# A decoder layer on one core: tile 2's first scores beside tile 1, the first block's last rows on ScalarE, tile 6's products before the rest of tile 7's scores

## The chip, the core and the metric

The kernel runs on one core of a Trainium2 chip. The core has five engines that work side by side, each through its own queue of instructions and in the order of that queue: TensorE (matrix products; PE in the profile, its weight loads PEld), VectorE (DVE), ScalarE (ACT), GpSimd (POOL) and SyncE (SP), which here only issues loads. An instruction waits at the head of its queue until the semaphores that it names have been raised by other engines or by transfers (DMA), and everything behind it waits too. The metric is the device time of one execution in microseconds (us), lower is better.

## What is computed

Two batches of 512 rows of 1024 features pass three sub-layers. Each adds its result to its input and normalises the row (mean 0, variance 1).

```
# attention per row over its own 32 x 32 (d, e) scores, 8 groups
q = einsum('bse,edh->bsdh', x, Wq) + bq ; k, v alike with 8 heads, repeated 4 times
scores = einsum('bsdh,bseh->bsde', q, k) / sqrt(32)
out = einsum('bsde,bseh->bsdh', softmax(scores), v).reshape(...)
x = _layernorm(x + out)
# product with the context, both rounded to 0..255 codes
q1, q2 = fake_quant(x, ...), fake_quant(ctx_4096, ...)
x = _layernorm(x + matmul(q1, q2))
# feed-forward: 2048 hidden columns, 512 latent ones scaled by the two largest gate values
h = relu(x @ up_w) ** 2 ; shared = h @ down_w
routed = ((x @ fc1_w) @ expert_w * sum(top2(x @ gate_w))) @ fc2_w
x = _layernorm(x + layernorm(shared + routed) * gamma + beta)
```

## The kernel before

**Tiles and blocks.** The 1024 rows are eight tiles of 128 rows, numbered 0 to 7 and written as `t`. Two tiles make a block. Blocks 0 and 1 each go through the feed-forward by themselves (`ffn`, then `down` for block 0 and `down_halved` for block 1). Blocks 2 and 3 go through it together (`ffn_pair`), with products that combine sums of operands so that fewer of them are needed.

**The token path of a tile** (`token_path`, a generator that pauses at each `yield`). `scores` makes the 32 x 32 scores of each row in four chunks: VectorE multiplies (L474, output `pqk`) and then adds over the groups (L480, output `s`). `exponentials` takes the largest (L489), subtracts it (L490) and has ScalarE take the exponent (L493). `attend` sums them (L499, `den`), multiplies with the values in four chunks (L507, `pav`), adds up (L513, `o`), divides (L518) and adds to the row (L528). The first normalisation follows. For tile 1 it is `normalise` on VectorE: statistics, one power on GpSimd (L330, `rstd`) and L336. For all others it is `normalise_aside` on ScalarE: `parts` (L346), a squared pass (L351), `ve` (L353), the power on GpSimd (L355), `shift` (L359) and the pass that writes the row (L360).

`cross` then makes the codes, on VectorE for tile 1 (`quantise`, L364 to L366) and on ScalarE for the others (`below_top` and L644, output `a`). TensorE turns the codes round (L652, or L630 for tile 1), ScalarE copies them (`aT`, L653), VectorE scales the row sum (L658, `r`) and adds a row of the context (L659). TensorE makes the product in two halves (L665, `py`), VectorE adds each to the row (L670) and the second normalisation follows. Between the codes and the turning, `cross` runs the generator `between`, which is what is left of the next tile's scores with their exponentials. `hand_over` turns the finished row tile round on TensorE (L134, `pt_x`), ScalarE copies it to `x2T` (L135), and GpSimd's queue adds beta to the row by a transfer (L737).

**The feed-forward.** In `ffn` each of the 16 products of a block (L827, `pu_c_i`) goes into one of two banks, and ScalarE empties the bank with `relu` (L843) and then squares (L844). Four latent products (`pl`) are copied (L856) and scaled on VectorE (L857). `down` accumulates 80 products (L1057) in four banks and at its end calls `finish` for each of the two tiles: on VectorE four `bn_stats` passes over the banks, two half-row passes (L1006) and one whole-row pass that adds the residual (L1013). A generator in `later` ends the row on ScalarE some steps afterwards (`store_aside`), and GpSimd's queue stores it (L1041). `beside` advances those generators.

**What sets the order.** The Python program takes turns between the token path, `fill` (projections and weight products before the first block) and `ffn` by weights that each `yield` hands back (`w_tok`, `w_ffn`, `PACE`). `tc.issue_after(ins)` adds an edge that puts an instruction behind another one on its engine. A scheduling layer then fixes one order for each engine and adds the semaphores. What a pool holds is given by its `bufs`: two banks for the products of `ffn`, two for turned tiles, two `prod` buffers, six row tiles `xc`.

Of the kernel before, what the change touches and what calls it, by code (L numbers as in the profile page):

```python
# [9 lines left out]
F32 = mybir.dt.float32  # L10
BF16 = mybir.dt.bfloat16
AF = mybir.ActivationFunctionType
ALU = mybir.AluOpType
# [14 lines left out]
def kernel(  # L28
# [286 lines left out]
        nc.sync.dma_start(gate[:, :, 0:NE], gate_w.rearrange("(k p) n -> p k n", p=P))  # L315
    gamma = const.tile([P, E], F32, name="gamma")

    def mean_rstd(halves, name, stats=None):
# [11 lines left out]
        nc.gpsimd.tensor_tensor(rstd, ve, neg_half, ALU.pow)  # L330
        return mv[:, 0:1], rstd

    def normalise(t, name):

        mean, rstd = mean_rstd([t[:, ts(h, HALF)] for h in range(E // HALF)], name)
        return nc.vector.tensor_scalar(t, t, mean, rstd, ALU.subtract, ALU.mult)  # L336

    def normalise_aside(t, sums, name):

# [22 lines left out]
    def quantise(dst, src, tmp, rs, z):  # L362

        nc.vector.tensor_scalar(tmp, src, rs, z, ALU.mult, ALU.add)  # L364
        nc.vector.tensor_scalar(tmp, tmp, 0.0, QMAX, ALU.max, ALU.min)
        nc.vector.tensor_scalar(dst, tmp, ROUND, ROUND + CENTRE, ALU.add, ALU.subtract)  # L366

    acted = [None]

# [94 lines left out]
            nc.gpsimd.dma_start(e2[ts(l, P), :], row)  # L464


    def scores(t, qk, behind=None):
        q3 = qk[:, 0:DG].rearrange("p (d g) -> p d g", g=G)
        k3 = qk[:, DG : 2 * DG].rearrange("p (e g) -> p e g", g=G)
        s = tokp.tile([P, D, D], F32, tag="s", name=f"s_{t}", bufs=2)  # L470
        for c in range(D // DC):
            prod = tokp.tile([P, DC * D * G], F32, tag="prod", name=f"pqk_{t}_{c}", bufs=2)
            with tc.issue_after(behind.ins) if behind is not None else ExitStack():
                nc.vector.tensor_tensor(  # L474
                    prod.rearrange("p (d e g) -> p d e g", d=DC, g=G),
                    q3[:, ts(c, DC), :].unsqueeze(2).to_broadcast([P, DC, D, G]),
                    k3.unsqueeze(1).to_broadcast([P, DC, D, G]),
                    ALU.mult,
                )
            nc.vector.tensor_reduce(  # L480
                s[:, ts(c, DC), :].rearrange("p d e -> p (d e)"),
                prod.rearrange("p (c g) -> p c g", g=G), AX.X, ALU.add,
            )
            yield 4.6
        return s

    def exponentials(t, s):
# [9 lines left out]
    def attend(t, xc, s, v):  # L497
        den = small.tile([P, D], F32, tag="den", name=f"den_{t}")
        nc.vector.tensor_reduce(den, s, AX.X, ALU.add)  # L499
        rden = small.tile([P, D], F32, tag="rden", name=f"rden_{t}")  # L500
        nc.vector.reciprocal(rden, den)
        yield 2.0

        o = tokp.tile([P, D, G], F32, tag="o", name=f"o_{t}")
        for c in range(D // DC):
            prod = tokp.tile([P, DC * D * G], F32, tag="prod", name=f"pav_{t}_{c}", bufs=2)
            nc.vector.tensor_tensor(  # L507
                prod.rearrange("p (d g e) -> p d g e", d=DC, g=G),
                s[:, ts(c, DC), :].unsqueeze(2).to_broadcast([P, DC, G, D]),
                v.unsqueeze(1).to_broadcast([P, DC, G, D]),  # L510
                ALU.mult,
            )
            nc.vector.tensor_reduce(  # L513
                o[:, ts(c, DC), :].rearrange("p d g -> p (d g)"),
                prod.rearrange("p (c e) -> p c e", e=D), AX.X, ALU.add,
            )
            yield 4.6
        nc.vector.tensor_tensor(o, o, rden.unsqueeze(2).to_broadcast([P, D, G]), ALU.mult)  # L518

        x3 = xc.rearrange("p (c j) -> p c j", j=J)  # L520
        o3 = o.rearrange("p d g -> p (d g)").unsqueeze(2).to_broadcast([P, DG, J])
        if t == TB - 1:

            nc.vector.tensor_tensor(x3, x3, o3, ALU.add)
# [91 lines left out]
    def cross(t, xc, cq, crow, between):  # L616
# [5 lines left out]
        aT = tokp.tile([P, KC, P], BF16, tag="aT", name=f"aT_{t}")  # L622
        if hurried:

            quantise(a, xc, tmp, rs1, z1)
            yield 2.2
            pt = ps_tr.tile([P, KC, P], BF16, tag="tr", name=f"pta_{t}")
            with behind_products():
# [11 lines left out]
        else:  # L640
# [12 lines left out]
            nc.scalar.copy(aT, pt)  # L653
            yield 4.0
        behind = ExitStack if hurried or t == NT - 1 else lambda: tc.issue_after(lowered[0].ins)
        r = small.tile([P, 1], F32, tag="r", name=f"r_{t}")
        with behind():
            nc.vector.tensor_mul(r, total, s12d2)  # L658
# [15 lines left out]
        if hurried:  # L674
            last = normalise(xc, f"2_{t}")
            yield 6.0
        else:
            yield 3.0
            last = yield from normalise_aside(xc, sums, f"2_{t}")
            yield 6.0  # L680
        return last

    def token_path():


        batch, last = None, None
        at, done = {}, {}

        def begin(t):
            xc = xpool.tile([P, E], F32, tag="xc", name=f"xc_{t}")  # L690
            nc.sync.dma_start(xc, xf[ts(t, P), :])
            qk, v = qkv.pop(t)
            if 0 < t < NT - 1:
                fetch_qkv(t + 1)
            at[t] = xc, v, scores(t, qk, last if t == TB else None)

        def scores_left(t):

# [10 lines left out]
        for blk in range(NBLK):  # L709
            xcs = []  # L710
            x2T = []
            for i in range(TB):
# [15 lines left out]
                last = yield from cross(t, xc, *batch, between)  # L728

                def hand_over(blk=blk, t=t, i=i, xc=xc, x2T=x2T):  # L730
                    if not x2T:
# [314 lines left out]
    def down(blk, h):  # L1046
# [524 lines left out]
```

## Time and profile before

| what | value |
|---|---|
| median of 3 runs | 699.16 us (698.65 to 702.17) |
| the profiled execution | 699.09 us, of which the span of the profile is 697.3 us |
| TensorE busy | 677.7 us (97%) |
| VectorE busy | 607.5 us (87%) |
| ScalarE busy | 263.7 us (38%) |
| GpSimd busy | 76.0 us (11%) |
| granted TensorE clock | 1.00 from 0 to 650 us, 0.90 from there to the end |
| moved by DMA | 139.08 MB, mean 199 GB/s |

The profile is one execution. A busy time is the sum of what an engine's instructions took. The matrix products overlap in a pipeline and their ends are worked out, so a busy TensorE need not be at its peak. Beside the totals there are tables of who waited for whom, a timeline of each engine, and busy times by stretch of the span. Three instants help to place what follows, all counted from the start of the span. The products of block 0's `ffn` begin at 143.46 us, those of block 1 at 297.21 us, and those of the pair at 454.64 us.

### The profile page before, as it was taken

How to read it: one execution, taken by the hardware profiler on the slowest of the kernel's cores; microseconds unless marked ns; L12 is line 12 of the kernel's file. 1: busy time of each engine (PE TensorE's matmuls, PEld its weight loads, DVE VectorE, ACT ScalarE, POOL GpSimd, SP SyncE). 2: the span in 40 equal slices, each digit the busy share in tenths (PEclk: the TensorE clock that was granted, in tenths of full speed). 3: DMA queues.
4: the chain of work that ended last, by engine and by line, in shares of the span. 5: the costliest groups of instructions: out<-in, count | busy, mean ns of one | idle time of the engine just before them, and what ended most of it. 6: DMA issues, size and time to landing. Idle time of an engine off the chain costs nothing.

```text
span 697.3 us, 7629 instructions
## 1 busy us (share of the span) xinstructions
PE 677.7 (97%) x2862; PEld 494.6 (71%) x2872; DVE 607.5 (87%) x724; ACT 263.7 (38%) x443; POOL 76.0 (11%) x107
## 2 busy tenths in 40 slices
PE   8999999999999999999999999999999999999991
PEld 4666654578877444478877458788888888888881
DVE  5899987699999999799999987698778679897895
ACT  1287543222635449627726215311144200000252
POOL 1012112200011122002001000020011000000012
PEclk9999999999999999999999999999999999999997
DMA  9999628394545548455535534695887545557733
GB/s 335 302 335 366 156 25 299 102 305 144 166 135 160 193 140 292 136 180 189 176 126 153 163 117 170 210 335 197 305 305 277 193 141 180 178 185 193 213 76 121
DMA packets 73460, 139.08 MB, mean 199 GB/s; under 512 B 5264, under 2 KB 39696, under 8 KB 73424
## 3 DMA queue, kind: packets, MB, share of 16 engines
q1 hardware_dynamic: 63216, 106.87, 45.3%
q0 software_dynamic: 10064, 31.47, 16.1%
q8 instruction: 22, 0.36, 0.2%
q10 hardware_dynamic: 144, 0.26, 0.1%
q14 instruction: 14, 0.11, 0.0%
HBM read 114.99 MB, written 21.50 MB: 196 GB/s over the span
## 4 chain that ended last, share of the span: by engine, by line
PE 46%; DVE 4%; ACT 3%; DMA 2%; issue 1%; POOL 1%; POOLq 0%; DVEq 0%; ACTq 0%
PE pp L942 9%; PE ps L1401 5%; PE pu L827 5%; PE pp_mm L942 5%; PE pd L1109 5%; PE ph L1129 4%; PE pp_tr L942 4%; PE ps_mm L1401 2%; PE pl L827 2%; PE ps_tr L1401 2%; PE py L665 1%; DMA dn<-tw 1%; ACT square L351 1%; DMA y_a<-xc 1%; DVE pav L507 1%
## 5 line engine op out<-in xcount | busy, mean ns | idle before, releaser
L827 PE MATMUL pu<-x2T,up 128*128 128x256 f32 x512 | 113.1, 380 | 0.8 <-ACT relu L843 0.8
L827 PEld LDWEIGHTS pu<-x2T,up 128*128 128x128 f32 x512 | 96.5, 190 | 14.9 <-ACT relu L843 1.2
L474 DVE TENSOR_TENSOR pqk<-qk 128x2048 f32<-128x2048 f32 x32 | 72.5, 2282 | 0.0
L507 DVE TENSOR_TENSOR pav<-s,v 128x2048 f32<-128x2048 f32 x32 | 72.4, 2281 | 0.0
L480 DVE TENSOR_REDUCE s<-pqk 128x256 f32<-128x2048 f32 x32 | 72.3, 2277 | 0.1
L513 DVE TENSOR_REDUCE o<-pav 128x64 f32<-128x2048 f32 x32 | 72.0, 2265 | 0.0
L1057 PE MATMUL pd<-dn,h 128*128 128x512 f32 x160 | 69.5, 593 | 0.0
L157 PE MATMUL pqk<-wqkv,xT 128*128 128x512 f32 x128 | 63.4, 595 | 0.9 <-DVE wqkv L249 0.6
L1057 PEld LDWEIGHTS pd<-dn,h 128*128 128x128 f32 x160 | 30.2, 190 | 36.2 <-issue 35.9
L162 PEld LDWEIGHTS pv<-wqkv,xT 128*128 128x128 f32 x128 | 24.3, 190 | 24.2 <-issue 22.5
L355 POOL TENSOR_TENSOR rstd<-ve,neg_half 128x1 f32<-128x1 f32 x21 | 19.7, 939 | 167.0 <-ACT ve L353 129.3
L162 PE MATMUL pv<-wqkv,xT 128*128 128x256 f32 x128 | 35.6, 379 | 0.0
L1109 PE MATMUL pd<-dn,h 128*128 128x512 f32 x80 | 35.0, 593 | 0.0
L843 ACT ACTIVATE relu<-pu 128x256 f32<-128x256 f32 x32 | 12.1, 377 | 52.1 <-PE pu L827 52.1
L157 PEld LDWEIGHTS pqk<-wqkv,xT 128*128 128x128 f32 x128 | 23.6, 190 | 11.1 <-issue 4.5
L1305 DVE TENSOR_TENSOR tt<-dn 128x1024 f32<-128x1024 f32 (+1 forms) x20 | 21.2, 1058 | 11.2 <-DMA dn<-in_L_ffn_down_w_dram 6.9
L665 PE MATMUL py<-cq,aT 128*128 128x512 bf16 x120 | 27.4, 379 | 1.5 <-ACT aT L653 1.1
L458 PE MATMUL pe<-fc,exT 128*128 128x512 f32 x64 | 28.7, 594 | 0.0
L827 PE MATMUL pl<-x2T,fc 128*128 128x256 f32 x128 | 28.0, 379 | 0.0
L1109 PEld LDWEIGHTS pd<-dn,h 128*128 128x128 f32 x80 | 15.0, 190 | 17.4 <-issue 17.2
L827 PEld LDWEIGHTS pl<-x2T,fc 128*128 128x128 f32 x128 | 24.3, 190 | 3.4
L665 PEld LDWEIGHTS <-aT 128*128 128x128 bf16 x128 | 12.4, 98 | 16.6 <-ACT aT L653 1.5
(338 smaller groups left out, 1274.6 us busy)
## 6 DMA issues: line engine op xcount, KB each, us to landing
up<-in_L_ffn_up_w_dram SPq DMA_DIRECT2D x16, 1024.0 KB, 5.4
dn<-in_L_ffn_down_w_dram SPq DMA_DIRECT2D x16, 1024.0 KB, 5.0
pair<-in_L_ffn_up_w_dram SPq DMA_DIRECT2D x8, 1024.0 KB, 6.7
dn<-tw SPq DMA_DIRECT2D x8, 1024.0 KB, 5.0
tw<-outer POOLq DMA_DIRECT2D x7, 1024.0 KB, 5.5
fc<-in_L_ffn_fc_w_dram SPq DMA_DIRECT2D x6, 1024.0 KB, 5.7
dn<-in_L_ffn_down_w_dram SPq DMA_DIRECT2D x12, 512.0 KB, 5.4
outer<-in_L_ffn_down_w_dram SPq DMA_DIRECT2D x5, 1024.0 KB, 5.4
```

The costliest lines, as they stand in the source:

```text
L157: projecting[0] = nc.tensor.matmul(pqk, xT[:, k, :], wqkv[k][:, 0 : 2 * DG], start=(k == 0), stop=(k == KE - 1))
L162: nc.tensor.matmul(pv[:, :DG], xT[:, k, :], wqkv[k][:, 2 * DG : 3 * DG], start=(k == 0), stop=(k == KE - 1),)
L474: nc.vector.tensor_tensor(prod.rearrange("p (d e g) -> p d e g", d=DC, g=G), q3[:, ts(c, DC), :].unsqueeze(2).to_broadcast([P, DC, D, G]), ...
L480: nc.vector.tensor_reduce(s[:, ts(c, DC), :].rearrange("p d e -> p (d e)"), prod.rearrange("p (c g) -> p c g", g=G), AX.X, ALU.add,)
L507: nc.vector.tensor_tensor(prod.rearrange("p (d g e) -> p d g e", d=DC, g=G), s[:, ts(c, DC), :].unsqueeze(2).to_broadcast([P, DC, G, D]), ...
L513: nc.vector.tensor_reduce(o[:, ts(c, DC), :].rearrange("p d g -> p (d g)"), prod.rearrange("p (c e) -> p c e", e=D), AX.X, ALU.add,)
L665: crossed[t] = nc.tensor.matmul(py, aT[:, k, :], cq[:, k, ts(h, HALF)], start=(k == 0), stop=(k == KC - 1))
L827: lately[0] = nc.tensor.matmul(ps[:, :NB], ws[:, k, wcols], xT[:, k, :], start=(k == 0), stop=(k == KE - 1))
L942: lately[0] = nc.tensor.matmul(banks[m], steps[g][m][:, k, :], moving[m][:, k, :], start=(k == 0 and m not in (6, 3, 7)), stop=(k == KH - ...
L1057: lately[0] = nc.tensor.matmul(pd[i][n], h[:, kk // 4, i, kk % 4, :], w[:, k, ts(n, HALF)], start=(kk == 0), stop=(kk == NK - 1),)
L1109: lately[0] = nc.tensor.matmul(pd[i], h[:, g, i, k, :], w[:, k, :], start=(g == 0 and k == 0), stop=(g == NG - 1 and k == 3),)
L1401: lately[0] = nc.tensor.matmul(banks[mm], unit(o, mm, j), inner_weights[o, cc][mm][:, j - lo, :], start=(j == 0 and mm not in FIRST_OF), s ...
```

## The change

Three parts of the token path and the feed-forward are moved, and one running total starts from another value.

1. Tile 2's scores are begun before tile 1's `attend` (`begin(TB)`). Their multiplications and additions are handed out one at a time: one multiplication behind the last step of tile 1's statistics and ahead of the pass that normalises, one addition and one multiplication behind the rounding of tile 1's codes and ahead of the scaling of its row sum. What is left comes behind tile 1's second normalisation, where all of it stood.
2. The rows of block 0 no longer go through `finish`. ScalarE copies the four banks and sums the rows as it does so, `normalise_aside` normalises, VectorE multiplies by gamma, a transfer on GpSimd's queue adds the residual into the row, ScalarE sums the row again, and `store_aside` ends it as before.
3. For tile 6, two chunks of tile 7's scores are run ahead of the turning of the codes, and the rest with the exponentials behind tile 6's second normalisation. The edge that held tile 6's row sum behind the next tile's subtraction (`lowered`) is dropped.
4. `w_tok` starts at 6.9 instead of 0.0 when the blocks begin.

```diff
-        nc.vector.tensor_scalar_add(ve, mv[:, 1:2], EPS)
+        measured[0] = nc.vector.tensor_scalar_add(ve, mv[:, 1:2], EPS)
...
-    def normalise(t, name):
+    def normalise(t, name, meanwhile=False):
...
-        return nc.vector.tensor_scalar(t, t, mean, rstd, ALU.subtract, ALU.mult)
+        with early_step(measured[0]) if meanwhile else ExitStack():
+            return nc.vector.tensor_scalar(t, t, mean, rstd, ALU.subtract, ALU.mult)
+
+    early, turn, stepped = [None], [None], [None]
+
+    def early_step(behind, n=1):
+        turn[0] = behind
+        for _ in range(n):
+            next(early[0])
+        return tc.issue_after(stepped[0].ins)
...
+            with tc.issue_after(turn[0].ins) if t == TB else ExitStack():
+                stepped[0] = nc.vector.tensor_tensor(
...
+            if t == TB:
+                yield 2.3
...
+            yield 2.3 if t == TB else 4.6
...
-            normalise(xc, f"1_{t}")
+            normalise(xc, f"1_{t}", True)
...
-            quantise(a, xc, tmp, rs1, z1)
+            rounded = quantise(a, xc, tmp, rs1, z1)
+            waited = early_step(rounded, 2)
...
-            yield from between
+            if t == NT - 2:
+                between = iter(between)
+                for _ in range(2):
+                    yield next(between)
+            else:
+                yield from between
...
-        behind = ExitStack if hurried or t == NT - 1 else lambda: tc.issue_after(lowered[0].ins)
+        behind = ExitStack if hurried or t >= NT - 2 else lambda: tc.issue_after(lowered[0].ins)
         r = small.tile([P, 1], F32, tag="r", name=f"r_{t}")
+        with waited if hurried else behind():
+            nc.vector.tensor_mul(r, total, s12d2)
         with behind():
-            nc.vector.tensor_mul(r, total, s12d2)
             nc.vector.scalar_tensor_tensor(xc, xc, r, crow, ALU.add, ALU.add)
...
             last = yield from normalise_aside(xc, sums, f"2_{t}")
+            if t == NT - 2:
+                yield from between
...
+                if t == TB - 1:
+                    begin(TB)
+                    early[0] = at[TB][2]
                 yield from attend(t, xc, done[t], v)
...
-            finish(blk, i, new_y(blk, i), pd[i])
+            y = new_y(blk, i)
+            sums = small.tile([P, 2], F32, tag="sum2_y", name=f"sum2_y_{blk}_{i}")
+            for n in range(2):
+                acted[0] = nc.scalar.activation(
+                    y[:, ts(n, HALF)], pd[i][n], AF.Copy, accum_out=sums[:, n : n + 1]
+                )
+            later.append(finish_aside(blk, i, y, sums))
+
+    def finish_aside(blk, i, y, sums):
+        yield
+        yield from normalise_aside(y, sums, f"f_{blk}_{i}")
+        yield
+        nc.vector.tensor_tensor(y, y, gamma, ALU.mult)
+        nc.gpsimd.dma_start(y, xcs_of[blk][i], accum_op=ALU.add)
+        yield
+        yield
+        sums = small.tile([P, 1], F32, tag="sum3", name=f"sum3_{blk}_{i}")
+        square = attp.tile([P, E], BF16, tag="square", name=f"summed_{blk}_{i}")
+        acted[0] = nc.scalar.activation(square, y, AF.Copy, accum_out=sums)
+        yield from store_aside(of[ts(blk * TB + i, P), :], y, sums, f"3_{blk}_{i}", 0)
...
-    w_tok, w_ffn, alive = 0.0, 0.0, True
+    w_tok, w_ffn, alive = 6.9, 0.0, True
```

The orders that the scheduling layer gives the two programs differ in these places. On TensorE there are as many instructions in both (1114), and the same until block 1's `down`: there tile 5's turned rows come after one product instead of two, and tile 6's codes are turned 12 products of 128x512 earlier, its context product beginning four products after that. On VectorE there are 12 instructions fewer, on ScalarE 16 more, on GpSimd's queue 2 more. On SyncE's queue two loads of up-weights stand ahead of the loads of the input rows of tiles 6 and 7 instead of between and behind them.

More of the change, by code (lines that the diff above doesn't have):

```diff
@@ L316 @@
     gamma = const.tile([P, E], F32, name="gamma")
+    measured = [None]
     def mean_rstd(halves, name, stats=None):
@@ L365, in quantise @@
         nc.vector.tensor_scalar(tmp, tmp, 0.0, QMAX, ALU.max, ALU.min)
-        nc.vector.tensor_scalar(dst, tmp, ROUND, ROUND + CENTRE, ALU.add, ALU.subtract)
+        return nc.vector.tensor_scalar(
+            dst, tmp, ROUND, ROUND + CENTRE, ALU.add, ALU.subtract
+        )
     acted = [None]
@@ L464, in fill, with scores @@
             nc.gpsimd.dma_start(e2[ts(l, P), :], row)
-    def scores(t, qk, behind=None):
+    def scores(t, qk):
         q3 = qk[:, 0:DG].rearrange("p (d g) -> p d g", g=G)
@@ L472, in scores @@
             prod = tokp.tile([P, DC * D * G], F32, tag="prod", name=f"pqk_{t}_{c}", bufs=2)
-            with tc.issue_after(behind.ins) if behind is not None else ExitStack():
-                nc.vector.tensor_tensor(
+            with tc.issue_after(turn[0].ins) if t == TB else ExitStack():
+                stepped[0] = nc.vector.tensor_tensor(
                     prod.rearrange("p (d e g) -> p d e g", d=DC, g=G),
@@ L479, in scores @@
                 )
[L480 to L484, printed above, removed]
+            if t == TB:
+                yield 2.3
+            with tc.issue_after(turn[0].ins) if t == TB else ExitStack():
+                stepped[0] = nc.vector.tensor_reduce(
+                    s[:, ts(c, DC), :].rearrange("p d e -> p (d e)"),
+                    prod.rearrange("p (c g) -> p c g", g=G), AX.X, ALU.add,
+                )
+            yield 2.3 if t == TB else 4.6
         return s
@@ L683, in token_path @@
     def token_path():
-        batch, last = None, None
+        batch = None
         at, done = {}, {}
@@ L694, in begin @@
                 fetch_qkv(t + 1)
-            at[t] = xc, v, scores(t, qk, last if t == TB else None)
+            at[t] = xc, v, scores(t, qk)
         def scores_left(t):
@@ L727, in token_path @@
                 between = scores_left(t + 1) if t + 1 < NT else ()
-                last = yield from cross(t, xc, *batch, between)
+                turn[0] = yield from cross(t, xc, *batch, between)
                 def hand_over(blk=blk, t=t, i=i, xc=xc, x2T=x2T):
@@ L1063, in down @@
         for i in range(TB):
-            finish(blk, i, new_y(blk, i), pd[i])
+            y = new_y(blk, i)
[3 more added lines that the diff above has]
+                    y[:, ts(n, HALF)], pd[i][n], AF.Copy, accum_out=sums[:, n : n + 1]
+                )
+            later.append(finish_aside(blk, i, y, sums))
[11 more added lines that the diff above has]
+        yield from store_aside(of[ts(blk * TB + i, P), :], y, sums, f"3_{blk}_{i}", 0)
     def down_halved(blk, h):
```

## The prediction

> **What bounds the kernel now.** I read the totals by engine, then the busy times by stretch (span, its length, then PE, PEld, DVE, ACT, POOL, each with its count, the granted clock, the DMA share, GB/s).
>
> ```profile
> PE 677.7 (97%) x2862; PEld 494.6 (71%) x2872; DVE 607.5 (87%) x724; ACT 263.7 (38%) x443; POOL 76.0 (11%) x107
> ```
> ```profile
> 0.00:50.00 50.00, 47.76 (x166) 27.69 (x167) 38.57 (x43) 21.77 (x27) 4.63 (x12) 1.00 0.94 325
> 50.00:650.00 600.00, 597.03 (x2547) 438.27 (x2556) 533.06 (x618) 222.74 (x377) 62.46 (x82) 1.00 0.61 195
> 650.00:697.30 47.30, 32.87 (x153) 28.59 (x151) 35.87 (x63) 19.21 (x40) 8.96 (x13) 0.90 0.40 124
> ```
>
> TensorE stands still for 19.6 us: 2.2 at the start, 14.4 in the last 47 us, which the change doesn't touch, and 600.00 - 597.03 = 2.97 between. Its instructions are the same before and after (1114), and their pitch is constant: 160 passes of block 0's up-products run from 157.74 to 192.36, 0.216 us each. So what this change can win is at most 2.97 us, 0.4%. What it can lose has no such bound: whatever reaches TensorE late adds in full. The table of waits names the stalls (total, count, longest).
>
> ```profile
> PE py L665 <- ACT aT L653: 1.1, 1, 1.1
> PE pu L827 <- ACT relu L843: 0.8, 1, 0.8
> PE pta L630 <- DVE a L366: 0.2, 1, 0.2
> ```
>
> The first is tile 2's (198 us), the second block 1's pu_3_0 (323 us), the third tile 1's codes (122.7 us). I followed each engine's new order by hand from these places, with one duration per kind of instruction: 2.28 us a multiplication of a score chunk, 2.20 its addition and all pitches between, an independent next operation 0.1 us before the end of the last, a dependent one 0.03 after.
>
> **Part 1, tile 2's early scores.** VectorE's two waits, and GpSimd's powers beside them:
>
> ```profile
> 119.54 0.81 DVE L336 TENSOR_SCALAR xc<-xc,mv,rstd 128x1024 f32<-128x1024 f32 x1 [3.08 <-POOL rstd L330]
> 127.04 0.16 DVE L658 TENSOR_TENSOR r<-pr,s12d 128x1 f32<-128x1 f32 x1 [4.38 <-PE pr L636]
> ```
> ```profile
> 118.41 0.57 POOL L355 TENSOR_TENSOR rstd<-ve,neg_half 128x1 f32<-128x1 f32 x1 [4.81 <-ACT ve L353]
> 118.96 0.54 POOL L330 TENSOR_TENSOR rstd<-ve,neg_half 128x1 f32<-128x1 f32 x1
> 228.11 2.10 POOL L355 TENSOR_TENSOR rstd<-ve,neg_half 128x1 f32<-128x1 f32 x1 [7.34 <-ACT ve L353]
> 336.75 0.56 POOL L355 TENSOR_TENSOR rstd<-ve,neg_half 128x1 f32<-128x1 f32 x1 [7.66 <-ACT ve L353]
> ```
>
> The first wait begins at 119.54 - 3.08 = 116.46; a multiplication ends at 118.74, inside it. An addition and a multiplication (4.40) just fill the 4.38 behind the rounding. Three operations, 6.6 us, leave the stretch before tile 2's softmax, and `den_2` starts at 148.6 instead of 155.2.
>
> A price is hidden in the power at L330. The one at 228.11 took 2.10 us: a multiplication of `pav` ran until 229.79, and the power ended 0.4 after it. At 336.75, beside an addition, it took 0.56. Tile 0's power (118.41) now meets pqk_2_0, ends about 118.74 + 0.5 = 119.25, and tile 1's follows at 119.8: 0.3 later. L336, the rounding and the turning at 122.7 follow, and TensorE already stands there for the codes: +0.3 (bounds 0 and 0.35; I take the row at 228.11, the same operand shapes beside the same kind of work).
>
> [...]
>
> What is won: with tile 2's softmax 6.6 us earlier, `exp_3` no longer stands between the turned codes and their copy on ScalarE; `aT_2` ends 0.8 us earlier and the stall of 1.1 falls to 0.27, by the 0.3 that a copy always leads its product. **-0.81.**
>
> The 6.6 us don't last. Tile 3's row sum waits for its codes, a chain on ScalarE that hangs on the latent copy at 218.5 and not on VectorE. Only its power is freed (0.56 for 2.10), and r_3 comes at 235.4 instead of 241.1. But the adds of py_3 now have three more chunk operations ahead of them (20.3 us behind r_3 instead of 13.7): they end at 257.15, before 256.27. From there ScalarE's `parts`, squared pass and row pass follow as before:
>
> ```profile
> 262.94 1.23 ACT L360 ACTIVATE xc<-xc,shift,rstd 128x1024 f32<-128x1024 f32 x1
> ```
> ```profile
> 264.32 1.04 PE L134 MATMUL pt_x<-ident,xc 128*128 128x128 f32 x8
> ```
>
> That pass now ends at 264.67 and the turning of tile 3 starts at 264.81, while TensorE is there at 264.32 - 0.81 = 263.51: a new stall, **+1.30**. Bounds: 0, if VectorE's queue is 1.3 us earlier than I add up, and 2.
>
> **Part 2, block 0's rows on ScalarE.** Four copies of banks (0.59 to 0.87 each, by the plain and the summing row of 128x512) fall into ScalarE's idle time before 301, when the first `relu` of block 1 is due. The second pair of row passes delays relu_1_0 to 311.2, and its bank is wanted at 315.9: hidden. VectorE loses four statistics and the `y` passes, some 8.7 us, and gains two multiplications by gamma (2.28). The transfers that add the residual start at 314.7 and 315.9. For their time there are these rows:
>
> ```profile
> y_a<-xc POOLq DMA_DIRECT2D x2, 512.0 KB, 4.5
> xc<-in_L_ffn_ln_beta_dram POOLq DMA_DIRECT2D x8, 512.0 KB, 7.1
> ```
>
> I take 4.5, a transfer between the same kinds of tiles, and 7.1 as the other end. The transfers then land at 319.6 and 320.7. ScalarE's summing passes wait for them, and behind these stand shift_4 and relu_2_0, which ends by 322.5. TensorE wants that bank at 322.83: no stall, and the 0.8 of before, which came from a late `relu`, is gone: **-0.81**. The slack is 0.3 us, and a landing beyond 4.9 us is paid in full. On SyncE's queue two up-weight loads now stand ahead of the loads of rows 6 and 7, whose buffers these transfers free some 13 us later than before. Row 6 is wanted at 358, so 30 us cover it; without that cover tile 6's residual, and with it its codes, would be late. The lead `w_tok` = 6.9 has its effect in the orders above and costs nothing by itself.
>
> **Part 3, and what it does to tile 5.** Tile 6's product comes 12 x 0.863 = 10.4 us earlier, near 400; its codes are ready at 390, so 10 us cover it. Dropping `lowered` delays nothing. But two chunks of tile 7 and its softmax move. `sub_7` now ends at 377.5 (before 387.65): tile 6's softmax is 9 us earlier, and tile 5's second-half adds (367.3), four chunk operations and the largest come before. ScalarE's new order has `exp_7` ahead of latent_1_1, parts_6 and the copy of tile 4's turned rows into `x2T`, and that copy frees the bank for tile 5's turning.
>
> ```profile
> 376.04 1.04 PE L134 MATMUL pt_x<-ident,xc 128*128 128x128 f32 x8
> 376.91 1.88 PE L1109 MATMUL pd<-dn,h 128*128 128x512 f32 x4
> 378.63 1.04 PE L134 MATMUL pt_x<-ident,xc 128*128 128x128 f32 x8
> ```
>
> Before, two product groups lay between the two turnings and nobody waited. Now one does, so TensorE is at the second turning at 375.88 + 0.87 + 0.86 = 377.61. ScalarE: exp_7 from 377.56 to 378.6, the copy from 378.97 to 379.55. **+2.04** (bounds 0, if sub_7 is ready 2 us earlier, and 3, with VectorE 1 us later).
>
> **The sum.** +0.30 - 0.81 + 1.30 - 0.81 + 2.04 = +2.0. The profiled execution took 699.09, its span 697.3 and 1.79 around it; the median of the runs is 699.16. Forecast: 699.09 + 2.0 = **701.1 us**, 0.3% above the median. With single terms at their bounds it goes from 699.8 to 702.4.
>
> **The rivals.**
> *Faster: both old stalls go and neither new one comes.* This holds if VectorE is about 2 us ahead of my sum at 257 and at 377. For it: VectorE issues fewer instructions (12 fewer) and 8.7 us of `finish` leave it. Against: in both places the order, not the load, decides; three chunk operations went ahead of py_3's adds. Time: 699.09 + 0.3 - 1.62 - 0.2 = 697.5 (the last for the codes' stall).
> *Slower: the transfers take 7.1 instead of 4.5.* Then summed_0 and summed_1 hold ScalarE's queue with relu_2_0 behind them, from 4.9 us on. Block 1's pu_3_0 stands 2.3 us, and exp_6, behind a `relu`, is as late and carries some of it to sub_7. Instead of nothing at 323 and +2.0 altogether it is +4.5: 703.6. At 6.0 us, as other adding transfers show, +2.5. For it: the loads of up-weights share the DMA engines there. Against: the row nearest in kind has 4.5.
> *The change does less than it says:* tile 2's early chunks give a lead that VectorE loses at the next wait for ScalarE, and tile 3's turning is where it was. Then 1.3 falls away: 699.8, inside the forecast's range.
>
> **How the numbers follow.** Forecast, with the third rival in it: 0.60. Faster rival: 0.15. Slower rival: 0.20. Something unforeseen: 0.05. A measurement of this kernel can tell about 0.5%, 3.5 us, from no change: below 695.7 is faster, above 702.7 slower. Faster: the 2.97 us of idle time exclude it but for a changed tail, 0.03. Slower: the slower rival (most of 0.20), the unforeseen and the forecast's upper edge, 0.24. Same: 0.73. The range reaches from the faster rival, less half a microsecond, 697.0, to the slower one with VectorE 0.9 later, 704.5; the likeliest case alone is 699.8 to 702.4.
>
> **What would show it.** In the profile after: `py` waiting for `aT` for 0.3 instead of 1.1; no `pu` waiting for `relu`; `pt_x` (L134 before) idle about 1.3 near 264 behind ScalarE's row pass, and about 2.0 near 379 behind `x2T`; `den_2` at 148.6; tile 0's power 0.8 long beside `pqk`; `sub_7` ending near 377.5. The prediction is wrong if TensorE's idle time between 50 and 650 is under 3 us (the faster rival) or if a `pu` waits over 1 us for `relu` with a summing pass ahead that waits for a transfer (the slower one), or if VectorE's busy time falls while its waits grow by as much.

## The result, and the profile after

The changed kernel took 708.68 us (median of 4 runs, 708.21 to 709.5) against 699.11 us for the kernel before beside it: a ratio of 1.0129 [1.0098, 1.0159], slower by 1.3%, 7.6 us above the forecast and 4.2 above its range. The profiled execution took 709.5 us, 10.4 more than that of before, and its span 707.7 against 697.3. All 10.4 us are accounted for below.

The totals by engine, of the changed kernel:

```profile
PE 679.4 (96%) x2862; PEld 495.4 (70%) x2872; DVE 602.5 (85%) x710; ACT 273.6 (39%) x469; POOL 73.0 (10%) x109
```

VectorE did 5 us less and ScalarE 10 us more, as the change means it. TensorE was busy 1.7 us longer with the same 2862 instructions, so some of them ran slower. The busy times by stretch, in the same columns as the prediction's:

```profile
0.00:50.00 50.00, 47.18 (x166) 27.36 (x167) 38.56 (x43) 21.83 (x27) 4.61 (x12) 1.00 0.92 325
50.00:650.00 600.00, 591.97 (x2513) 432.94 (x2522) 520.91 (x592) 232.72 (x403) 58.18 (x83) 0.99 0.60 194
650.00:707.70 57.70, 40.24 (x187) 35.08 (x185) 42.99 (x76) 19.09 (x40) 10.18 (x14) 0.88 0.44 128
```

TensorE's idle time between 50 and 650 us went from 2.97 to 600.00 - 591.97 = 8.03 us, and its mean clock there from 1.00 to 0.99. The table of waits (total, count, longest) names the place:

```profile
PE pu L856 <- ACT relu L872: 5.0, 1, 5.0
...
PE pt_x L134 <- ACT xc L372: 1.1, 1, 1.1
...
PE pt_x L134 <- ACT x2T L135: 0.5, 1, 0.5
PE pta L648 <- DVE a L378: 0.4, 1, 0.4
...
PE py L689 <- ACT aT L676: 0.3, 1, 0.3
```

The last four answer to the forecast's steps. The first is the slower rival's place, at more than twice its price. ScalarE's timeline there (start, duration, operation, in brackets the idle time before it and who ended it):

```profile
319.78 1.06 ACT L1112 ACTIVATE summed<-y 128x1024 bf16<-128x1024 f32 x1 [1.05 <-DMA y<-xc]
...
326.49 1.06 ACT L1112 ACTIVATE summed<-y 128x1024 bf16<-128x1024 f32 x1 [5.56 <-DMA y<-xc]
```

And the chain of waits of the same kernel (start, us, what):

```profile
315.32 11.08 DMA y<-xc
...
326.49 1.15 ACT summed L1112 x2
327.64 0.18 ACT shift L371
327.82 0.28 ACT relu L872
...
328.14 6.88 PE pu L856 x22
```

The reader sees one transfer of 11.08 us, a summing pass that waited 5.56 us for it at the head of ScalarE's queue, behind it the little `shift` and the `relu` that empties a bank, and TensorE's next product at 328.14. The product in that bank had been finished since 319.67 and TensorE stood from 323.12; nothing but the order of the queue tied the `relu` to the transfer.

A second loss follows at once, in the busy times by stretch (the clock is the third number from the end):

```profile
325.00:330.00 5.00, 1.86 (x4) 1.51 (x5) 5.00 (x6) 3.48 (x8) 0.00 (x0) 0.51 0.69 226
330.00:335.00 5.00, 5.00 (x20) 4.27 (x19) 1.90 (x4) 4.97 (x14) 1.22 (x3) 0.80 0.52 182
```

The granted clock was halved from 325.13 to 331.96 us. TensorE worked again from 328.14, so its first 3.8 us ran at half speed (9 passes in 3.82 us, and 20 in the 4.04 behind them) and cost 1.9.

The third loss is at the end. One line of VectorE's timeline, of the changed kernel:

```profile
659.99 0.69 DVE L1395 SCALAR_TENSOR_TENSOR y_a<-y_a,y_b 128x512 f32<-128x512 f32 x1 [4.01 <-DMA y_a<-p]
```

and of the kernel before:

```profile
648.22 0.69 DVE L1346 SCALAR_TENSOR_TENSOR y_a<-y_a,y_b 128x512 f32<-128x512 f32 x1 [0.42 <-DMA y_a<-p]
```

The transfer `y_a<-p`, which the change doesn't touch, took 9.6 us instead of 6.0.

By TensorE's products, after less before, the 10.4 us add up like this:

| from, to (product) | before, us | after, us | shift | what came in |
|---|---|---|---|---|
| block 0's first product | 143.46 | 143.51 | +0.05 | |
| `py` of tile 2 | 199.08 | 198.30 | -0.78 | old stall gone |
| turning of tile 3 (`pt_x`) | 264.32 | 264.78 | +0.46 | new stall, 1.08 |
| block 1's `pu_3_0` | 323.41 | 328.14 | +4.73 | 5.02 for 0.81: +4.2 |
| first `pw` | 351.14 | 357.74 | +6.60 | half clock: +1.9 |
| first `ph` | 416.08 | 423.44 | +7.36 | tile 5's turning: +0.76 |
| last product | 682.28 | 689.64 | +7.36 | |
| end of the span | 697.3 | 707.7 | +10.4 | slow transfer: +3.0 |

### The profile page after: what moved, and what is told of

Its sections match the earlier page's. It is cut to its first block, busy times and chain, and to the rows that moved or that the text cites. A ratio compares the mean times of both kernels' runs of the same rounds, so it can differ in the third digit from the quotient of the medians.

```text
span 707.7 us, 7650 instructions
## 1 busy us (share of the span) xinstructions
PE 679.4 (96%) x2862; PEld 495.4 (70%) x2872; DVE 602.5 (85%) x710; ACT 273.6 (39%) x469; POOL 73.0 (10%) x109
## 4 chain that ended last, share of the span: by engine, by line
PE 75%; DVE 7%; ACT 6%; issue 5%; DMA 4%; POOL 1%; SPq 0%; POOLq 0%; DVEq 0%; ACTq 0%
PE pu L856 14%; PE pp L971 9%; PE pqk L157 8%; PE pp_mm L971 5%; PE pd L1158 5%; PE ph L1178 4%; PE ps L1450 4%; PE pd L1086 4%; PE pv L162 4%; PE pp_tr L971 4%; PE pe L472 3%; PE py L689 3%; PE ps_mm L1450 2%; PE ps_tr L1450 2%; DMA y<-xc 2%
## 5 line engine op out<-in xcount | busy, mean ns | idle before, releaser
L856 PE MATMUL pu<-x2T,up 128*128 128x256 f32 x512 | 115.0, 385 | 5.0 <-ACT relu L872 5.0
L367 POOL TENSOR_TENSOR rstd<-ve,neg_half 128x1 f32<-128x1 f32 x21 | 14.4, 687 | 173.3 <-ACT ve L365 170.0
```

Of the source, the lines that this page charges most:

```text
L856: lately[0] = nc.tensor.matmul(ps[:, :NB], ws[:, k, wcols], xT[:, k, :], start=(k == 0), stop=(k == KE - 1))
```

## The experiments

Four sets: which part costs, what in the transfers costs, whether the forecast's own steps are real, and the tail. Each ratio is to runs of the kernel before taken beside it, whose median was 699.4 to 700.3 us.

**1. Part 2 undone.** In the changed kernel:

```diff
-            y = new_y(blk, i)
...
-            later.append(finish_aside(blk, i, y, sums))
+            finish(blk, i, new_y(blk, i), pd[i])
```

> The changed kernel with part 2 undone (block 0's rows end on VectorE as before; parts 1, 3 and 4 stay). Both theories: the loss at 323 goes, the 0.8 of before may be back: 708.7 - 4.2 - 1.9 = 702.6, or 699.6 if the 3 us of the last stretch came with the stall. If part 2 is not what costs, it stays over 706.

Measured: 698.85 us (698.14 to 699.02, 10 runs), 0.9979 [0.9969, 0.9989]. Its table of waits:

```profile
PE pt_x L134 <- ACT xc L372: 1.1, 1, 1.1
...
PE pta L648 <- DVE a L378: 0.4, 1, 0.4
...
PE py L689 <- ACT aT L676: 0.3, 1, 0.3
```

No `pu` waits, the clock isn't halved there, and `y_a<-p` takes 6.6. So part 2 is worth some 10 us, and the rest of the change gains a little, less than a measurement of this kernel tells from no change by the bound of the prediction.

**2. Part 2 alone**, put into the kernel before (the rows of `finish` replaced as in the change, nothing else).

> The kernel before with part 2 alone (block 0's rows on ScalarE with the two transfers). Held queue: the same two transfers 1.1 us apart are enough; a pu waits 3 to 6 us, 703 to 707. Rival (parts together): the transfers meet the up-weight loads only in the order that parts 1 and 4 make; no wait over 1.5, 698 to 701.

Measured: 706.49 us (705.34 to 707.21, 4 runs), 1.009 [1.0072, 1.0107].

```profile
PE pu L827 <- ACT relu L843: 5.4, 1, 5.4
```

The stall needs no other part. Here the transfers start three microseconds later (317.51 and 318.64) with no load issued between them, and take 5.4 and 7.6; the later start makes up for the shorter time. The half clock lasts 3.4 us. The tail's transfer is as in the kernel before (5.9).

**3. ScalarE's queue let past the transfer.** In the changed kernel the summing pass comes 12 turns of the generator later instead of 2, so that the four `relu` passes due meanwhile stand ahead of it:

```diff
-        yield
-        yield
+        for _ in range(12):
+            yield
         sums = small.tile([P, 1], F32, tag="sum3", name=f"sum3_{blk}_{i}")
```

> The changed kernel with one edit: the two passes on ScalarE that sum block 0's rows wait 12 steps instead of 2, so that relu_2_0 to relu_3_1 stand ahead of them; the transfers stay. Theory (held queue): the 5.0 us that pu_3_0 waits is ScalarE's queue held by summed_1, which waits 11 us for y_1's transfer; with it goes the halved clock behind the wait (1.9 us). No pu waits over 1 us, no half clock near 325, 708.7 - 5.0 - 1.9 = 701.8, and 698.8 if the 3 us of the last stretch go with it. Rival (load): it is ScalarE's added work of some 10 us that makes the relu late; a pu still waits 3 us or more and the time stays over 706.

Measured: 704.61 us (702.78 to 707.02, 6 runs), 1.0068 [1.0048, 1.0089]. The `relu` passes came in time, at 320.48 and 323.00, yet TensorE still waited:

```profile
PE pu L856 <- DMA up<-in_L_ffn_up_w_dram: 2.9, 1, 2.9
```

The queue explains the 5.0 us of the changed kernel, but behind it lies a second wait that I had not priced: the up-weights `up_3`, issued at 315.65, landed at 325.76, after 10.1 us, where the median of the 16 loads of `up` in this kernel is 5.4. The transfers and the load hold each other up. This wait of 2.9 us was followed by no half clock in the profiled execution, which at 702.78 is the fastest of the six.

**4. The residual without a transfer.** VectorE adds it and sums the row in the same instruction:

```diff
-        nc.gpsimd.dma_start(y, xcs_of[blk][i], accum_op=ALU.add)
...
+        nc.vector.scalar_tensor_tensor(
+            y, y, 1.0, xcs_of[blk][i], ALU.mult, ALU.add, accum_out=sums
+        )
...
-        acted[0] = nc.scalar.activation(square, y, AF.Copy, accum_out=sums)
```

> The changed kernel with the residual of block 0 added on VectorE, which sums the row in the same pass, instead of the two transfers and the two summing passes on ScalarE. Held queue: no transfer to wait for, pu waits at most 1, 701 to 703 (698 to 700 if the last stretch goes back too); VectorE has 2.6 us more near 316, which may add up to 2 at tile 5's turning. Load: ScalarE loses only 2.5 of its 10 us, a pu still waits about 3, 705 or more.

Measured: 699.96 us (698.97 to 702.24, 10 runs), 1.0009 [0.9997, 1.0021]. The wait for `relu` is 0.6 (0.8 before the change). What is left of part 2, the copies of the banks and the normalising on ScalarE with the addition on VectorE, costs some 1 us by the medians against experiment 1 and 2 by the ratios; what costs most is the transfers with the passes behind them.

**5. One transfer instead of two.** As 4, for the second row alone (`if i == 0` keeps the transfer).

> The changed kernel with only row tile 0 of block 0 getting its residual by a transfer; tile 1's is added on VectorE, which sums the row too. Theory (shared DMA engines): y_1 took 11.1 us because it ran behind y_0 and up_3's load. Alone, y_0 lands 5.5 us after its issue, up_3's load is no later than before, and no pu waits over 1 us: 699 to 702. Rival (each adding transfer is slow by itself beside a load of weights): y_0 takes 8 us or more, summed_0 still holds ScalarE's queue, a pu waits 2 us or more, 703 or more.

Measured: 701.62 us (700.43 to 702.98, 10 runs), 1.0017 [1.0004, 1.0030]. The one transfer took 5.1 us, the load came 0.7 late at most, nobody waited for `relu`.

**6. to 8. The load between the transfers.** In the changed kernel `up_3` is issued at 315.80, half a microsecond behind the second transfer. In 6 it is left out and the third part of the weights used again; in 7 its first eighth alone is loaded; in 8 all of it goes on GpSimd's queue, behind both transfers.

```diff
+            if (blk, c) != (1, 3):      # 6
...
+            few = 1 if (blk, c) == (1, 3) else KE      # 7
+            nc.sync.dma_start(w[:, 0:few, :], up3[:, 0:few, ts(c, CW)])
...
+            queue = nc.gpsimd if (blk, c) == (1, 3) else nc.sync      # 8
+            queue.dma_start(w, up3[:, :, ts(c, CW)])
```

> The changed kernel without the load of block 1's fourth part of the up-weights (up_3); its products use the third part again, so the values differ. Theory (order of issue on shared DMA engines): y_1 took 11.1 us because up_3's 1 MB, issued between the two transfers, ran between them. Without it y_1 lands 7.5 to 8 us after its issue, as in rows_alone, near 323.3 instead of 326.5; a pu waits about 2 instead of 5, no half clock follows, 708.7 - 3.2 - 1.9 = 703.6 (2 to 3 more or less by the last stretch). Rival (the second adding transfer is slow by itself or by the load of row 6 that y_0 frees): y_1 still takes 10 us or more, a pu waits over 4, 707 or more.

Measured: 708.74 us (707.2 to 708.83, 4 runs), 1.0125 [1.0107, 1.0143]. A miss: with no `up_3` to wait for, SyncE's next load, `up_4`, went out at 315.69 in its place, as large, and the second transfer took 11.8 us. It told nothing apart.

> The changed kernel with up_3 cut to an eighth: 128 KB instead of 1 MB are loaded and its products use that eighth for all eight blocks of rows, so the values differ. The buffer is held as before, so no other load takes its place (in no_load up_4 did). Theory (the load ran between the transfers): y_1 lands 7.5 to 8 us after its issue, near 323.3; a pu waits 2 to 2.6 instead of 5.0, no half clock or a shorter one; 703 to 705. Rival (the second adding transfer is slow whatever lies between): y_1 takes 10 us or more, a pu waits over 4, 707 or more.

Measured: 701.39 us (701.22 to 703.7, 6 runs), 1.0038 [1.0023, 1.0053]. The second transfer lasted from 315.30 to 322.11, 6.8 us, less than the 7.5 to 8 that I expected. ScalarE's summing pass, then TensorE's product, of this kernel:

```profile
322.19 1.06 ACT L1113 ACTIVATE summed<-y 128x1024 bf16<-128x1024 f32 x1 [1.91 <-DMA y<-xc]
```
```profile
323.85 16.48 PE L856 MATMUL pu<-x2T,up 128*128 128x256 f32 x75 [0.74 <-ACT relu L873]
```

With the load cut, the pass waits 1.91 us instead of 5.56 and the product 0.74 instead of 5.02.

> The changed kernel with up_3's whole load issued on GpSimd's queue, behind the two transfers, instead of on SyncE's between them. Theory: y_1 takes 7.5 to 8 us and ScalarE's queue is free at 324, but the load now comes last of the three and lands near 327, so a pu waits 4 to 5 us for the load instead of for relu: the wait changes its releaser and not its size, 706 to 709. Rival: y_1 still takes 10 us or more and the releaser is still relu.

Measured: 705.24 us (703.02 to 706.25, 4 runs), 1.0084 [1.0059, 1.0110]. The second transfer took 7.5, the `relu` came in time, and the load, issued at 315.51, landed at 325.93. The order came out as expected, the wait and the time below their ranges:

```profile
PE pu L856 <- DMA up<-in_L_ffn_up_w_dram: 3.5, 1, 3.5
```

Taken together: the first transfer takes 4.8 to 5.7 us, the second 6.8 to 7.6 behind it, and 10.8 to 11.8 where SyncE's issue of a 1 MB load begins 0.3 to 0.5 us behind its own. In 8 the same load stands behind it in GpSimd's queue and the transfer takes 7.5, so it is not the load as such but its getting in ahead. Where ScalarE's queue is free (3 and 8), the load lets TensorE wait 2.9 to 3.5 us by itself. Neither order that was tried serves both waiters at this place; less traffic does (4, 5 and 7).

**9. The lead set back to zero** (part 2 undone, and `w_tok` = 0.0 as before the change).

```diff
-    w_tok, w_ffn, alive = 6.9, 0.0, True
+    w_tok, w_ffn, alive = 0.0, 0.0, True
```

> The kernel 'changed without part 2' (698.85) with w_tok starting at 0.0, as in the kernel before. Theory: the 6.9 only keeps the products of tile 2's codes where they were; without it TensorE turns them one product earlier, may wait up to 2 us for them, and py_3's adds come elsewhere in VectorE's queue: 698.5 to 701. Rival (the lead is what gains): over 701.

Measured: 702.56 us (700.91 to 704.51, 5 runs), 1.0047 [1.0028, 1.0066], 0.7% above experiment 1 by the ratios and 3.7 us by the medians (of which 0.9 is in the kernel before beside it, 700.33 for 699.41). TensorE's and ScalarE's timelines of this kernel:

```profile
379.39 1.15 PE L134 MATMUL pt_x<-ident,xc 128*128 128x128 f32 x8 [1.78 <-ACT x2T L135]
```
```profile
377.54 1.06 ACT L510 ACTIVATE s<-s 128x1024 f32<-128x1024 f32 x1 [4.70 <-DVE s L507]
```

This is the stall that I forecast at tile 5's turning, with its cause: `exp_7` ahead of the copy into `x2T`. The lead, which I priced at nothing, takes it away in experiment 1. With part 2 it doesn't: experiment 7, which has the lead and hardly waits at 323, waits 1.28 us here. The profiled execution (700.91 us) is the lowest of the five and its span 1.9 us above that of experiment 1, which the waits account for; where the rest of the runs' difference lies no profile shows.

**10. Parts 1 and 4 alone**, put into the kernel before.

> The kernel before with parts 1 and 4 alone (tile 2's early scores, and the running total from 6.9). By the prediction's terms: aT's wait -0.8, tile 3's turned rows +1.1 to 1.3, the power +0.1 to 0.3: 698.5 to 700. If part 3 is what made 'changed without part 2' faster, this is over 699.5; if not, it is near 698.9.

Measured: 698.46 us (698.18 to 701.62, 10 runs), 0.9986 [0.9975, 0.9998], not to be told from experiment 1. Part 3 brings nothing that can be measured beside these two.

**11. and 12. Against the stall at tile 3's turning** (both on experiment 1). In 11 the first multiplication of tile 5's scores and the last addition of tile 4's values are put behind `py_3`'s adds by edges; in 12 the first passes over context rows 3 and 4 go behind tile 3's row pass:

```diff
+            after = turn if t == TB else tokens_added if (t, c) == (5, 0) else None      # 11
...
+            if b == 1 and k in (3, 4):      # 12
...
+                with tc.issue_after(turned_3[0].ins):
+                    next(passes[k])
```

> The kernel 'changed without part 2' (698.85) with two edges that keep one multiplication of tile 5's scores and the last addition of tile 4's values behind py_3's two adds. Theory (order of VectorE's queue): the adds start at 253.9 instead of 256.0 and the 1.1 us that TensorE waits for tile 3's turned rows go: 697.7. Rival (ScalarE's context passes set that row's end): the wait stays at 0.8 or more, 698.5 to 699.2.

Measured: 699.13 us (698.74 to 701.57, 11 runs), 0.9994 [0.9982, 1.0005].

> The kernel 'changed without part 2' with two edges on ScalarE: the first passes over context rows 3 and 4 of the second batch stand behind tile 3's row pass instead of ahead of it. Theory (ScalarE's context passes keep tile 3's row): the row pass ends near 262.5 instead of 264.9, TensorE's wait of 1.1 us before tile 3's turning goes, 698.85 - 1.1 = 697.7. Rival (the context is late for it): the context row's product at 286 waits for its codes by as much, 698.5 to 699.5.

Measured: 701.38 us (700.43 to 704.19, 12 runs), 1.0026 [1.0011, 1.0040]. Both are misses. The adds came at 253.4 and the row pass ended at 262.7, as meant, but the scheduling layer moved the turning forward on TensorE as well, to 263.97 and 262.76, and it waited 1.4 and 1.3 us. In 12 a `pu` also waited 1.8 us for `relu`. The row passes show that the stall isn't VectorE's lateness alone: with the adds 2.6 us earlier (11) the pass ended 1.0 us earlier than in experiment 1 (263.92 for 264.93), because passes over context rows filled ScalarE's queue; with two of those moved behind it (12) it ended 2.2 earlier, the adds where they were.

**13. to 15. The tail.** On experiment 1, two small operations on GpSimd ahead of `y_a<-p` were to delay its issue: in 13 they read a part of the sum that is ready early, in 14 the part written last. 15 is the changed kernel again, unedited. The lines of 14:

```diff
+                held_up = small.tile([P, 1], F32, tag="held_up", name="held_up", bufs=1)
+                nc.gpsimd.tensor_tensor(held_up, c12[:, 0, 0:1], neg_half, ALU.mult)
+                nc.gpsimd.tensor_tensor(held_up, held_up, neg_half, ALU.mult)
```

> The kernel 'changed without part 2' (698.85) with two small GpSimd operations, 0.55 us each, between VectorE's last addition to the running sum and the transfer y_a<-p of the last stretch. Theory (order of issue): 1.1 us later, the transfer comes behind the 1 MB load dn<-tw on the same DMA engines, takes 9 to 10 us instead of 6.6, VectorE waits 4 us or more for it, and the end is 2 to 4 us later: 701 to 703. Rival (only its own delay): VectorE waits at most 1.1 us more, 698.9 to 700.

Measured: 698.5 us (698.27 to 701.35, 10 runs), 0.9979 [0.9964, 0.9993]. A miss: the operations were over before the transfer was due.

> As late_issue, whose two small operations read a part of the sum that was ready early and so delayed nothing; these read the part that is written last. Theory (order of issue): the transfer y_a<-p is issued 1 us later, behind the load dn<-tw, takes 9 us or more, VectorE waits 4 us or more for it and the end is 2 to 4 us later: 701 to 703. Rival (only its own delay): VectorE waits 1 us more, 698.9 to 700.

Measured: 698.54 us (697.97 to 701.14, 10 runs), 0.9988 [0.9974, 1.0003]. In the profiled execution (700.33 us) the issue came 0.3 us nearer to that of the next load than in experiment 1 (0.72 against 1.04, see the table below), and that was enough for most of the loss:

```profile
651.19 0.69 DVE L1389 SCALAR_TENSOR_TENSOR y_a<-y_a,y_b 128x512 f32<-128x512 f32 x1 [3.65 <-DMA y_a<-p]
```

Four of its ten runs lie at 699.76 or above, the other six at 698.6 or below, so by the median the expected 701 to 703 is a miss.

> The changed kernel once more, nothing edited. If the last stretch is lost by the change itself, y_a<-p takes 9 us or more again and VectorE waits 4 us for it. If it is chance, it takes 6 to 7 and the span is 3 us shorter than 707.7. The wait at pu_3_0 should be 4.5 to 5.5 in both, and the half clock 0 to 2 us beside it; 705 to 709.

Measured: 710.0 us (707.1 to 711.18, 4 runs), 1.0138 [1.0115, 1.0161]. All three losses recur: 5.1 us for `relu`, 6.8 us of half clock, `y_a<-p` 9.6 and VectorE 4.03. The median is a microsecond above what I expected, because TensorE worked through 6.0 us of the half clock (328.40 to 334.40), which cost 3 us instead of up to 2.

What decides the tail shows when the profiles are put in order of one figure, the time from the start of the issue of `y_a<-p` to the start of that of SyncE's next load of 1 MB (`dn<-tw`):

| kernel | that margin, us | transfer, us | VectorE waits, us |
|---|---|---|---|
| experiment 8 | 1.93 | 5.8 | 0.28 |
| before | 1.47 | 6.0 | 0.42 |
| experiment 6 | 1.19 | 6.4 | 0.86 |
| experiment 1 | 1.04 | 6.6 | 1.07 |
| experiments 13, 5 | 0.84 | 7.1 | 1.56, 1.46 |
| experiment 14 | 0.72 | 8.7 | 3.65 |
| the changed kernel | 0.65 | 9.6 | 4.01 |
| experiment 12 | 0.64 | 9.3 | 3.73 |
| experiment 15 | 0.53 | 9.6 | 4.03 |

The seven profiles left out (margins 1.17 to 1.73) have 5.8 to 6.4. Between 0.84 and 0.72 the time of the transfer jumps. That is where the order in which the two issues end turns round: GpSimd's issuing instruction for `y_a<-p` took 1.18 to 1.20 us in all 17 profiles, SyncE's for the load 0.36, so at a margin under some 0.83 the load is out first.

The margin itself hangs on an earlier load. VectorE begins this stretch when a load of 512 KB (`dn<-in_L_ffn_down_w_dram`), issued some 13 to 14 us ahead of `y_a<-p`, lands. The margin and that load's time add up to 7.94 or 7.95 us in twelve profiles. They add up to 7.59 or 7.60 in the changed kernel, 15, 6 and 7, where VectorE also stands 0.46 us ahead of `dn<-dn,tt`, and to 7.44 in 14. The load took 6.48 us in the kernel before, 6.95 in the changed one and 7.06 in 15; why it takes longer there stays open. Experiment 12 and the profiled execution of 14 lost the margin without part 2, and 2 kept it with part 2. So the 3 us can't be put down to the change's own instructions; that they go with the changed kernel rests on its two profiles alone.

## Why the prediction was wrong, point by point

**The step that failed** is the price of the transfers: "I take 4.5, a transfer between the same kinds of tiles, and 7.1 as the other end. The transfers then land at 319.6 and 320.7." The first landed at 319.8, after 5.6 us; the second at 326.4, after 11.1. The row of 4.5 is of two transfers that ran alone: in the kernel before they were issued at 664.36 and 669.11, the second after the first had landed and both after the last load (663.73). And I gave the second transfer the first one's time. Experiment 7 prices what I left out: with the load cut to an eighth the second takes 6.8. So about 2.3 us are the first transfer ahead of it (6.8 against 4.5) and 4.3 the rest of the load (11.1 less 6.8). Neither end of my bounds held the value, because both came from rows of the transfer itself and none from what was issued beside it. The prediction named that load only as an argument for the rival.

**The slower rival was the right mechanism.** It said that a summing pass would hold ScalarE's queue with relu_2_0 behind it, from 4.9 us on. That is the place, the order and the cause in the profile. At 7.1 us it priced 2.3 us of wait; at 11.1 the wait is 5.02. Experiments 3 and 4 confirm it: passing the queue brings 1.3% down to 0.7%, no transfer brings it to 0.1%. But it was too small in two ways. It had no place for the load as a second waiter (2.9 us in experiment 3), and none for the clock.

**The half clock** (+1.9) was no step of the prediction; a stall was priced at its length. Here a wait of 5.02 cost 6.9, and in experiment 15 one of 5.11 some 8.

**-0.81 at `py` of tile 2** held: 0.3 us of wait remain, the shift went from +0.05 to -0.78, `den_2` started at 148.66 against a forecast of 148.6.

**+0.30 at the codes** was too much: +0.1. Tile 0's power did take 0.68 (0.8 forecast), beside the multiplication that ended at 118.60. But that multiplication ended 0.14 earlier than I had it and the power 0.43 after it, so tile 1's followed at 119.02 instead of 119.25 or later, and L336 (now L339) started at 119.59 instead of 119.54. One reading was wrong there: what ran beside the power at 228.11 were two multiplications of scores (`pqk`, 225.31 to 229.79) and none of `pav`. The price doesn't change by it.

**+1.30 at tile 3's turning**: the turning started at 264.78, forecast 264.81, and waited 1.08, TensorE coming 0.2 later than I had it. The time of the step was right. Its working is right in part: VectorE's adds end where I had them (257.23), but experiments 11 and 12 show that the context passes ahead of the row pass on ScalarE hold the row as well, and they moved the waiter too. The third rival, by which this stall wouldn't come, is refuted.

**-0.81 and no stall at `pu_3_0`**: +4.2, the failed step.

**+2.04 at tile 5's turning**: +0.76 between the two products around it, of which the wait is 0.49. The order was as forecast, `exp_7` ahead of the copy. `exp_7` started at 383.08, which less TensorE's shift of 6.6 is 376.5, and 376.4 in experiment 3 (379.06 less 2.7), where I had 377.56. So `sub_7` was 1.1 us earlier than my sum. And TensorE comes late to it, after the 6.6 us lost before; where it doesn't, in experiment 7, the wait is 1.28. Experiment 9 shows the stall at nearly its full size (1.78) without the lead; "costs nothing by itself" missed that the lead gains 0.7% by the ratios.

**The tail at nothing**: +3.0. I saw idle time there that the change doesn't touch and took it as fixed. It hangs on which of two issues ends first.

**The loads of rows 6 and 7**, which I covered with 30 us, made no wait; SyncE issued them at 319.83 and some 7 us later. The faster rival needed neither new stall to come; both came (1.08 and 0.49), and the first stays in experiment 1, which at 698.85 is still above that rival's 697.5.

## What to carry over

The transfers of one kind here, 512 KB each, took 4.5, 6.8 and 11.1 us, by what was issued beside them. So before taking a duration from a row, write down every transfer and load issued within a few microseconds of it, in the order in which their issues end, and add them up. And before a pass that waits for a transfer is put on an engine's queue, list what stands behind it there; a product whose operands had long been ready waited 5 us for a sum that nobody needed yet. The version of experiment 1, with the early scores and the lead and without part 2, is faster than the kernel before by 0.2% [0.1, 0.3], and faster than the changed one by about 1.5%.

## What the hardware showed that I had not expected

**Transfers of different queues ran one after the other.** The view of transfers of the changed kernel between 310 and 330 us gives the rate in forty slices of half a microsecond (GB/s):

```profile
GB/s 0 0 0 0 0 0 0 0 0 0 0 131 262 172 188 123 74 98 227 365 350 307 289 231 248 303 207 223 256 279 287 361 287 8 33 123 303 385 260 217
...
y<-xc POOLq DMA_DIRECT2D x2, 512.0 KB, 8.3
```

The last line gives the two transfers' median, 8.3 us from issue to landing (5.6 and 11.1). The rate is 74 to 262 until 319 and 365 to 289 just after. By the records of single packets the first transfer's run from 315.7 to 319.4, the load's from 319.0 to 324.2, nearly all of them by 323, and the second transfer's from 321.9 to 325.9. The second transfer's issue began half a microsecond before the load's, but took GpSimd from 315.32 to 316.19; SyncE's took from 315.80 to 316.16 and was over first. So they ran almost one after the other, in the order in which their issues ended, and the table of margins agrees: the transfers whose issue began 0.53 to 0.72 us before the load's took 8.7 to 9.6 us, those at 0.84 or more 5.8 to 7.1.

**A stall cost more than its wait.** In the changed kernel TensorE stopped at 323.12; 2.0 us later the granted clock was halved, for 6.83 us (325.13 to 331.96), and the wait of 5.02 cost 6.9. Other runs that waited at this place differ in what came with it: in experiment 15 a wait of 5.11 us brought 6.8 us of half clock, in experiment 2 one of 5.4 brought 3.4, from 5.3 us after the stop, in experiment 8 one of 3.5 brought 3.4, and in experiment 3 one of 2.9 brought none. The longest of these waits had half as much of the half clock as those of 5.02 and 5.11, so the length of a wait does not settle by itself what it costs; what else does isn't shown here.
